# A fused two-layer network on one core: the triangle's b projection read by rows, its output in four row groups, gate logits joined, and the whole order drawn up anew

## The chip, the cores and the metric

The kernel runs on one core of a Trainium2 chip. A core has five engines that run their own queues of instructions in order: TensorE (PE) multiplies matrices and transposes, with its weight loads shown apart as PEld; VectorE (DVE) and ScalarE (ACT) work on tiles; GpSimd (POOL) here issues indirect DMAs; SyncE (SP) issues most other DMAs. Matmuls write to PSUM, which has eight banks of 512 floats per partition. The metric is the time of one execution in microseconds on the device. Before the change three runs took 4004.34 to 4016.94 us, with a median of 4013.66.

## The reference

The input x has 32 images of 56 x 56 pixels with 128 channels. Everything is float32. Two layers follow each other, each with a mixing part and an expert part, both added to x.

```python
x = x + conv3x3(sign(batchnorm(ln(x))), sign(W) * scale)   # layer 0
t = t + moe8_top2(ln(t))                                   # 8 experts of 128x128, two per token
# layer 1, the "triangle", with n = ln(x), per image:
a = sigmoid((n @ Wa1 + ba1) * (n @ Wa2 + ba2))             # 16 channels
b = sigmoid((n @ Wb1 + bb1) * (n @ Wb2 + bb2))
z = einsum('bikc,bkjc->bijc', a, b)
x = x + sigmoid(n @ Wg + bg) * (ln(z) @ Wz + bz)
# 64 experts, each picks its 8 best tokens of an image
probs = softmax(ln(t) @ gate_w.T + gate_b, over tokens)
topv, topi = top_k(probs, 8)
pooled = sum_k topv[k] * ln(t)[topi[k]]                    # one row per image and expert
o = gelu([pooled, 1] @ weight1) @ weight2                  # 128 -> 512 -> 128
t[topi[k]] += topv[k] * o                                  # scatter
```

## The kernel before

A first sweep reads all of x in 112 units of 896 tokens (7 per pair of images), normalizes, and collects the batch norm's sums. After that the kernel works by pairs of images: 16 pairs, each 7 units of 16 image rows, two half units of 8 rows (448 pixels) in each.

Per unit it runs the convolution (nine taps, `ps_cv`, L595), the eight small experts (`acc`, L794, on gates broadcast by SP and multiplied by DVE at L789), and a normalized, transposed copy `yT` of the pair. Transposes of all kinds go through one helper, `turned` (L439).

Then comes the triangle, once per pair. `gated_half` (L839) projects `yT` for a and for b: two halves, two images, four column groups of 32 outputs. For a the moving operand is seven whole image rows. For b it is seven image columns, so that consecutive elements lie a row (56 floats) apart. Each makes one PSUM bank (`ps_a`, `ps_b`) of 392 columns, read out by ACT (L846). After a transpose and the product of both projections, `tri_z` multiplies a and b per channel (`ps_z`, L929) and normalizes. Its result `zT` has, on 128 partitions, eight neighbouring image columns times 16 channels.

`tri_out` works per unit. It makes the gate (`ps_g`, L992, a sigmoid on ACT, L1002) and the output projection `ps_zo` (L1020): eight matmuls, four in each of two row groups of 64 partitions, against weights `wz_bd` in which only 16 rows of each block are not zero. Two PSUM banks receive them, each with four image columns. Two DVE instructions of 448 elements (L1030) add the bias and multiply by the gate.

Gate logits (L1084) come in seven chunks of 448 tokens per image; two images go side by side in one bank, with 64 experts each. Chunks 0 and 6 were split by image, so that nine PE steps served a pair. Then `top8` finds each expert's tokens on DVE (L1111, L1115), POOL gathers their rows (L1153), and `pool_rows` sums them.

The 64 large experts run in 16 groups of four at the end. A group loads about 2 MB of weights, does three PE steps (`ph` L1338, `trh` L1351, `po` L1365), spreads the result to tokens (`pe` L1391), multiplies by the gains on DVE (`eo`, L1400), and POOL scatters it: four experts times two lots of images, one indirect DMA each (L1417). A scatter must wait for the one before it in its lot. The first `LATE` groups run before the last pair is pooled, without it ("False" in tile names), and again alone for the last pair ("True"); the other groups run once for all.

No loop fixes the order of instructions. Every stage declares operations with an engine, an estimated duration in ns, and what they read and write. A planner in Python (`Order.run`) simulates the engines and picks for each the ready operation of the lowest rank; the emitted order is then fixed. Rank is a tick given in `plan` (`put`, `late`), 14 ticks to a pair. `AHEAD` limits how far a tile may run ahead of its turn for a buffer, `SPARE` how many must be left over.

Of the kernel before, what the change touches and what calls it, by code (L numbers as in the profile page):

```python
# [54 lines left out]
class Order:  # L55
# [11 lines left out]
    AHEAD = {"u": 14, "ps": 32}  # L67
# [64 lines left out]
    def run(self):  # L132
# [18 lines left out]
        def can(k):  # L151

            need = {}
            for t in ops[k][5]:
                if t not in slot:
                    need.setdefault(t.args[1], []).append(t)
            for tag, tiles in need.items():
                spare = sum(1 for f in free[tag] if f <= now) - len(tiles)
                if tag not in heads:
                    heads[tag] = list(  # L160
                        itertools.islice(
                            (t for t in self.queue[tag][turn[tag] :] if t not in slot),
                            self.AHEAD.get(tag, 6),
                        )
                    )
                head = heads[tag]

                if spare < (0 if set(head[: len(tiles)]) == set(tiles) else self.SPARE.get(tag, 1)):
                    return False
                if any(t not in head for t in tiles):  # L170
                    return False
            return True

        def pick(e):

            kept, best = [], None
            while ready[e]:
                item = heapq.heappop(ready[e])
# [5 lines left out]
                kept.append(item)  # L184
            for item in kept:
                if item is not best:
                    heapq.heappush(ready[e], item)
# [5 lines left out]
        while len(out) < n:  # L193
# [47 lines left out]
            while events and events[0][0] <= now:  # L241
                k = heapq.heappop(events)[1]
                if k >= 0:
                    heapq.heappush(ready[ops[k][0]], (ops[k][6], k))
# [9 lines left out]
def kernel(ctx: ExitStack, tc: tile.TileContext, a: dict, out: bass.AP):  # L254
# [40 lines left out]
    wz_bd = const.tile([128, NV // 2, C], F32, name="wz_bd")  # L295
# [77 lines left out]
    with ExitStack() as c2:  # L373
# [54 lines left out]
        def turned(src, name, keys=None, get=None):  # L428
# [4 lines left out]
            for n0, k in ((0, 4), (4, 3)):  # L433
                ps = bank(f"{name}_{n0}")

                @op("PE", k * 109, r=keys or parts(src)[n0 : n0 + k], w=[ps])
# [144 lines left out]
        def conv(p, u):  # L581
            g = p * NU + u
            cv = live[p]["cv", u] = unit_tile(f"cv_{g}")
            for h in range(2):
# [5 lines left out]
                @op("PE", 9 * 194, r=near, w=[ps])  # L590
# [59 lines left out]
        def moe_route(p, m):  # L650
# [12 lines left out]
            @op("PE", 870, r=[k for xT in xTs for k in parts(xT)], w=[psl])  # L663
# [14 lines left out]
            @op("PE", 440, r=[rT], w=[psr])  # L678
# [93 lines left out]
        def moe_experts(p, u, n):  # L772
# [18 lines left out]
            @op("PE", 222 * E0, r=[gb], w=[(acc, n % 4)])  # L791
# [37 lines left out]
        def gated_half(p, x, h, pieces, w, bias):  # L829


            name = f"{x}_{p}_{h}"
            for img in range(2):
                ps = bank(f"ps_{name}_{img}")

                @op("PE", 760, r=all_rows, w=[ps])
                def _(ps=ps, img=img):
                    for g in range(4):
                        nc.tensor.matmul(  # L839
                            ps.ap[32 * g : 32 * g + 32, :392].rearrange("s (i k) -> s i k", i=7),  # L840
# [4 lines left out]
                def _(ps=ps, img=img):  # L845
                    nc.scalar.activation(  # L846
                        lines[h][:, :, 64 * img : 64 * img + H],
                        ps.ap[:, :392].rearrange("s (i k) -> s i k", i=7),
# [24 lines left out]
        def tri_b(p, h):  # L873

            if h == 0:
# [4 lines left out]
                lambda img, g: yT[:, H * img : H * img + H, 14 * g + 7 * h : 14 * g + 7 * h + 7]  # L880
                .rearrange("c k j -> c j k"), wb, bb,
# [1007 lines left out]
```

## Time and profile before

| | |
|---|---|
| median of three runs | 4013.66 us |
| the profiled execution | 4013.14 us |
| its span, first to last instruction | 4011.4 us |
| mean granted PE clock | 0.960 |
| busy: PE, DVE, ACT, POOL | 3678.5, 3143.3, 2348.2, 418.2 us |
| ps_b, 512 matmul instructions | 102.0 us busy |
| ps_a, 512 matmul instructions | 60.7 us busy |
| ps_zo, 1792 matmul instructions | 130.6 us busy |
| gate logits, 448 matmul instructions | 131.1 us busy |
| gate product on DVE, 224 instructions | 150.2 us busy, 680 ns each |
| scatters on POOL, 128 | 198.9 us busy, 1554 ns each |

A float32 matmul shows as two instructions, so 512 instructions of ps_b are 256 matmuls. Busy time of a group is the union of its instructions; they overlap on PE, so that the mean length of one is longer than its share. A line of groups ends with the idle time just ahead of it and with whom the engine waited for. A time such as 3570.05 is counted from the start of the span.

### The profile page before, as it was taken

To read this page: it belongs to the slowest core of one execution; us is meant where nothing else is said; L and a number is where in the kernel's file an instruction comes from. 1 tells how busy PE (TensorE), PEld (TensorE's weight loads), DVE (VectorE), ACT (ScalarE), POOL (GpSimd) and SP (SyncE) were. 2 spreads that over 40 slices of the span, in tenths; PEclk is the share of its full clock that TensorE was granted. 3 is DMA by queue.
4 is the path that set the end of the run, shared out by engine and by line. 5 is a ranking of instruction groups with operands and counts; after the bars stand their busy time and mean duration, and the time that the engine had idled before them with its cause. 6 is when DMAs were issued, how large, how long until landed. Compare 5 with 4: busy or idle time off the path is not lost.

```text
span 4011.4 us, 78057 instructions
## 1 busy us (share of the span) xinstructions
PE 3678.5 (92%) x27747; PEld 2896.2 (72%) x27747; DVE 3143.3 (78%) x10284; ACT 2348.2 (59%) x5461; POOL 418.2 (10%) x441
## 2 busy tenths in 40 slices
PE   6998999999999999999999999999999999988574
PEld 6886877777777777776877777777778686865352
DVE  7997878797978797978888989797888788865310
ACT  5997347475656565656666665656474756555210
POOL 1000000101010001010101010101000101004655
PEclk8999999999999999999999999999999999988687
DMA  7996546373746464645555555555555555457685
GB/s 241 349 353 230 213 143 251 132 263 130 256 139 238 148 246 149 235 155 202 193 193 192 198 195 194 189 195 193 198 181 210 185 206 186 175 183 223 178 246 130
DMA packets 316805, 814.11 MB, mean 203 GB/s; under 512 B 72168, under 2 KB 96608, under 8 KB 316416
## 3 DMA queue, kind: packets, MB, share of 16 engines
q1 hardware_dynamic: 253296, 682.59, 49.0%
q10 hardware_dynamic: 41104, 109.20, 6.9%
q0 software_dynamic: 22016, 17.32, 2.8%
q8 instruction: 221, 3.62, 0.4%
q14 instruction: 168, 1.38, 0.1%
HBM read 638.78 MB, written 170.13 MB: 202 GB/s over the span
## 4 chain that ended last, share of the span: by engine, by line
PE 65%; ACT 10%; DMA 10%; DVE 8%; POOL 3%; issue 3%; SPq 1%; ACTq 0%; POOLq 0%; DVEq 0%
PE acc L794 31%; PE ps_cv L595 6%; DMA out<-eo_False,picked 4%; PE gram L1593 3%; PE ps_g L992 2%; PE ps_zo L1020 2%; PE ps_b L839 2%; PE ps_l L1084 2%; DMA rows<-y,near 2%; PE tr L439 2%; DMA gb<-gate 2%; ACT yt L524 2%; PE tro L439 2%; DVE gb L789 2%; PE trm L439 2%
## 5 line engine op out<-in xcount | busy, mean ns | idle before, releaser
L794 PEld LDWEIGHTS acc<-expert_w,gb 128*128 128x128 f32 x12544 | 1448.6, 195 | 99.7 <-DVE gb L789 32.0
L794 PE MATMUL acc<-expert_w,gb 128*128 128x128 f32 x12544 | 1471.8, 279 | 48.8 <-DVE gb L789 37.8
L789 DVE TENSOR_TENSOR gb<-gb,xT 128x1024 f32<-128x1024 f32 x784 | 944.3, 1221 | 80.1 <-DMA gb<-gate 73.9
L450 DVE BATCH_NORM_STATS2 stln<-x 128x6 f32<-128x128 f32 x2352 | 589.3, 286 | 2.5
L1153 POOL DMA_INDIRECT rows<-y,near x128 | 185.9, 1452 | 3396.6 <-PE trm L439 1681.0
L595 PE MATMUL ps_cv<-frame,w_sign 128*128 128x448 bf16 x2016 | 419.0, 356 | 7.1 <-DVE frame L573 7.1
L524 ACT ACTIVATE yt<-x,rmln 128x128 f32<-128x128 f32 x784 | 322.5, 484 | 160.7 <-DVE rmln L509 157.6
L524 ACT ACTIVATE ym<-x,rmln 128x128 f32<-128x128 f32 x784 | 326.8, 490 | 95.0 <-DVE rmln L512 81.4
L524 ACT ACTIVATE yl<-x,rmln 128x128 f32<-128x128 f32 x784 | 326.9, 486 | 33.6 <-DVE rmln L509 18.3
L595 PEld LDWEIGHTS <-w_sign 128*128 128x128 bf16 x2016 | 193.5, 98 | 185.7 <-issue 21.0
L603 ACT ACTIVATE cv<-ps_cv,cv_shift,cv_scale 128x448 f32<-128x448 f32 x224 | 161.4, 723 | 99.3 <-PE ps_cv L595 93.1
L1417 POOL DMA_INDIRECT out<-eo_False,picked x128 | 198.9, 1554 | 179.3 <-DMA out<-eo_False,picked 108.1
L545 ACT COPY xT<-trm 128x512 f32<-128x512 f32 x224 | 112.1, 542 | 179.5 <-PE trm L439 145.5
L524 ACT ACTIVATE y<-x,rm 128x128 f32<-128x128 f32 x448 | 195.2, 491 | 24.8 <-DVE rm L509 11.8
L806 DVE TENSOR_TENSOR x<-acc,x 128x512 f32<-128x512 f32 x224 | 139.4, 622 | 77.2 <-PE acc L794 76.5
L992 PE MATMUL ps_g<-yT,wg 128*128 128x448 f32 x448 | 199.6, 554 | 0.0
L1593 PE MATMUL gram<-y 128*128 128x128 f32 x1568 | 199.5, 281 | 0.0
L545 ACT COPY ylT<-trl 128x512 f32<-128x512 f32 x224 | 111.4, 534 | 147.2 <-PE trl L439 141.8
L1593 PEld LDWEIGHTS gram<-y 128*128 128x128 f32 x1568 | 195.9, 201 | 0.0
L450 DVE BATCH_NORM_STATS2 st<-x 128x6 f32<-128x128 f32 x784 | 180.0, 280 | 16.6 <-DMA x<-in_x 16.0
L1030 DVE SCALAR_TENSOR_TENSOR sg<-ps_zo,bz,sg 128x448 f32<-128x448 f32 x224 | 150.2, 680 | 43.4 <-PE ps_zo L1020 40.6
L1002 ACT ACTIVATE sg<-ps_g,bg 128x448 f32<-128x448 f32 x224 | 137.3, 634 | 69.2 <-PE ps_g L992 39.2
(229 smaller groups left out, 5449.8 us busy)
## 6 DMA issues: line engine op xcount, KB each, us to landing
gb<-gate SPq DMA_DIRECT2D x784, 512.0 KB
x<-in_x SPq DMA_DIRECT2D x224, 448.0 KB
y<-yT SPq DMA_DIRECT2D x112, 448.0 KB
ys<-y SPq DMA_DIRECT2D x112, 448.0 KB
out<-x ACTq DMA_DIRECT2D x112, 448.0 KB
y<-yl ACTq DMA_DIRECT2D x112, 448.0 KB
w_False<-in_L_ffn_weight SPq DMA_DIRECT2D x128, 256.0 KB
w_True<-in_L_ffn_weight SPq DMA_DIRECT2D x80, 256.0 KB
```

Source lines behind the costliest of these rows:

```text
L439: nc.tensor.transpose(ps.ap[:, n * 128 : (n + 1) * 128], get()[:, n0 + n, :], ident)
L450: nc.vector.bn_stats(st.ap[:, c0 + k, :], src.ap[:, k, :])
L524: nc.scalar.activation(dst.ap[:, k, :], src.ap[:, k, :], AF.Identity, bias=m, scale=r)
L545: nc.scalar.copy(t.ap[:, n0 : n0 + k, :].rearrange("c n p -> c (n p)"), ps.ap[:, : k * 128],)
L595: nc.tensor.matmul(acc, lhsT=w_sign[:, tap, :], rhs=frames[f][:, 8 * band + kh : 8 * band + kh + 8, kw : kw + W], start=(tap == 0), stop=( ...
L603: nc.scalar.activation(cv.ap[:, :, 64 * h : 64 * h + 64], ps.ap[:, :448].rearrange("c (q n) -> c n q", n=N7), AF.Identity, bias=cv_shift, ...
L789: nc.vector.tensor_tensor(gb.ap, gb.ap, over(xT.ap[:, n, :], E0), ALU.mult)
L794: nc.tensor.matmul(acc.ap[:, n % 4 * C : (n % 4 + 1) * C], lhsT=gb.ap[:, e, :], rhs=expert_w[:, e * C : (e + 1) * C], start=(e == 0), stop ...
L992: nc.tensor.matmul(psg.ap[:, :448], lhsT=wg, rhs=yT[:, H * img + r0 : H * img + r0 + 8, :].rearrange("c r w -> c (r w)"), start=True, stop ...
L1153: nc.gpsimd.indirect_dma_start(out=rows.ap[:, j, :], out_offset=None, in_=y3_d[p], in_offset=bass.IndirectOffsetOnAxis(ap=near.ap[:, k + j ...
L1417: ins = nc.gpsimd.indirect_dma_start(out=tokens_out, out_offset=bass.IndirectOffsetOnAxis(ap=picked[lot][:rows, e : e + 1], axis=0), in_=e ...
L1593: nc.tensor.matmul(gram.ap[:, :C], lhsT=y.ap[:, n, :], rhs=y.ap[:, n, :], start=(g % G16 == 0 and n == 0), stop=(g % G16 == G16 - 1 and n ...
```

## The change

The change has five parts.

1. For b, `gated_half` reads image rows of seven neighbouring columns (56 runs of seven floats) instead of seven columns. The bank's columns then come in another order, and ACT's readout turns them back.
2. `ps_zo` is split in four row groups of 32 partitions with a bank each: again eight matmuls, two in each group. DVE's product becomes four instructions of 224 elements.
3. Chunk 0 of the gate logits is done for both images at once.
4. The estimated PE durations are longer, but for `ps_zo`'s; POOL's indirect DMAs are estimated slower; `AHEAD` is smaller; most ticks move, and the late ticks of the last pair are scaled by 0.94.
5. `LATE` is 6 instead of 10, with other ticks for the late groups.

The planner's bookkeeping is rewritten too (a sorted list in place of a heap, an earlier test of `AHEAD`).

```diff
-    AHEAD = {"u": 14, "ps": 32}
+    AHEAD = {"u": 12, "ps": 31}
...
-                @op("PE", k * 109, r=keys or parts(src)[n0 : n0 + k], w=[ps])
+                @op("PE", k * 125, r=keys or parts(src)[n0 : n0 + k], w=[ps])
...
-                @op("PE", 9 * 194, r=near, w=[ps])
+                @op("PE", 9 * 200, r=near, w=[ps])
...
-            @op("PE", 870, r=[k for xT in xTs for k in parts(xT)], w=[psl])
+            @op("PE", 1100, r=[k for xT in xTs for k in parts(xT)], w=[psl])
...
-            @op("PE", 222 * E0, r=[gb], w=[(acc, n % 4)])
+            @op("PE", 227 * E0, r=[gb], w=[(acc, n % 4)])
...
-                @op("PE", 760, r=all_rows, w=[ps])
+                @op("PE", 830, r=all_rows, w=[ps])
                 def _(ps=ps, img=img):
                     for g in range(4):
                         nc.tensor.matmul(
-                            ps.ap[32 * g : 32 * g + 32, :392].rearrange("s (i k) -> s i k", i=7),
+                            ps.ap[32 * g : 32 * g + 32, :392].rearrange(
+                                "s (i k) -> s i k", k=7 if cols else H
+                            ),
                             lhsT=w, rhs=pieces(img, g), start=True, stop=True,
...
-                        ps.ap[:, :392].rearrange("s (i k) -> s i k", i=7),
+                        ps.ap[:, :392].rearrange("s (k i) -> s i k" if cols else "s (i k) -> s i k", i=7),
...
-                lambda img, g: yT[:, H * img : H * img + H, 14 * g + 7 * h : 14 * g + 7 * h + 7]
-                .rearrange("c k j -> c j k"), wb, bb,
+                lambda img, g: yT[:, H * img : H * img + H, 14 * g + 7 * h : 14 * g + 7 * h + 7],
+                wb, bb,
...
-            psz = [bank(f"ps_zo_{name}_{h}") for h in range(2)]
-
-            @op("PE", 4 * 230, r=[(zT, 0), (zT, 4), (sg, "s", 0)], w=psz)
+            psz = [bank(f"ps_zo_{name}_{q}") for q in range(4)]
+
+            @op("PE", 750, r=[(zT, 0), (zT, 4), (sg, "s", 0)], w=psz)
...
-                for v in range(4):
-                    for h in range(2):
-                        k = slice(64 * h, 64 * h + 64)
-                        acc = psz[h].ap[:, :448].rearrange(
-                            "c (n r v) -> c v n r", n=N7, v=4
+                for v in range(2):
+                    for q in range(4):
+                        k = slice(32 * q, 32 * q + 32)
+                        acc = psz[q].ap[:, :224].rearrange("c (n r v) -> c v n r", n=N7, v=2)
+                        nc.tensor.matmul(
+                            acc[:, v], lhsT=wz_bd[k, v, :], rhs=z_[k], start=True, stop=True,
+                            **({"tile_position": (96, 0)} if q == 3 else {}),
                         )
...
-            for h in range(2):
-                @op("DVE", 600, r=[psz[h], (sg, "s", 0), (sg, "s", 1)],
+            for q in range(4):
+                @op("DVE", 320, r=[psz[q], (sg, "s", 0), (sg, "s", 1)],
...
-            ((0, (1,)), (6, (0,))), ((0, (0,)), (1, (0, 1))), ((2, (0, 1)), (3, (0, 1))),
+            ((6, (0,)),), ((0, (0, 1)), (1, (0, 1))), ((2, (0, 1)), (3, (0, 1))),
...
-        LATE = 10
+        LATE = 6
...
-                        "POOL", 1500, land=2400,
+                        "POOL", 1650, land=2900,
...
+        SHRINK = {NP - 2: 1, NP - 1: 0.94}
...
-                    put(t + 0.15 * n, moe_experts, p, u, n)
+                    put(t + 0.05 * n, moe_experts, p, u, n)
...
-                put(16.5 + 0.53 * u, tri_turn, p, u)
+                put(16.67 + 0.53 * u, tri_turn, p, u)
...
-                put(20.09 + 0.2 * h, tri_b, p, h)
+                put(19.99 + 0.2 * h, tri_b, p, h)
...
-            t = 22.99
+            t = 22.81
...
-                    t += 0.84
+                    t += 1.02
...
-            put(t + 3.83, top8, p)
-            put(t + 7, pool_rows, p)
+            put(t + 3.51, top8, p)
+            put(t + 6.06, pool_rows, p)
+        first_at, last_at = (at(p, t + 7) for p in (NP - 2, NP - 1))
...
             if g < LATE:
-                late(t + 7.5 + 0.5 * g, late_experts, True, g)
-        late(t + 7.4, last_sums)
-        late(t + 14, last_out_rows)
+                late(first_at + 0.5 + 1.35 * g, late_experts, False, g)
+                late(last_at + 0.1 + 1.53 * g, late_experts, True, g)
+            else:
+                late(last_at + 0.1 + 0.68 * (g - LATE), late_experts, False, g)
```

## The prediction

> **What bounds the kernel now.** I read the page's busy shares and slices first. TensorE (PE) is busy 92% of the span, 9 tenths in nearly every slice at nearly full clock, until the last four slices, where it drops and GpSimd (POOL) rises.
>
> ```profile
> PE 3678.5 (92%) x27747; PEld 2896.2 (72%) x27747; DVE 3143.3 (78%) x10284; ACT 2348.2 (59%) x5461; POOL 418.2 (10%) x441
> PE   6998999999999999999999999999999999988574
> POOL 1000000101010001010101010101000101004655
> PEclk8999999999999999999999999999999999988687
> ```
>
> Then busy time by stretch. The first gather of pooled rows marks each pair of images: pair 0 at 705.2 us, pair 14 at 3570.05, so a pair costs 2864.85/14 = 204.6 us. The rows below (stretch, length, busy us of PE, PEld, DVE, ACT, POOL, clock, DMA share, GB/s) are this steady part, the last pair up to its own gathers (A), its gathers (B), the rest (C).
>
> ```profile
> 705.20:3570.05 2864.85, 2740.16 (x21032) 2164.09 (x21030) 2424.64 (x7499) 1750.82 (x3914) 167.94 (x112) 0.98 0.54 192
> 3570.00:3762.00 192.00, 150.65 (x945) 96.20 (x946) 83.74 (x262) 92.50 (x173) 86.90 (x104) 0.84 0.72 205
> 3762.00:3805.00 43.00, 16.13 (x71) 9.39 (x68) 14.37 (x28) 3.03 (x4) 33.44 (x40) 0.60 0.66 171
> 3805.00:4011.40 206.40, 119.45 (x761) 81.46 (x761) 26.88 (x65) 18.96 (x33) 118.76 (x161) 0.81 0.70 184
> ```
>
> Per pair, PE works 195.7 us of 204.6, DVE 173.2: PE is the bound, with 8.9 us idle. In C nothing on PE is near full. There the chain of waits is made of the indirect scatters of expert outputs; each waits for the one before in its lot, and two lots alternate.
>
> Last I read prices in the chain of waits (start, us, what). It runs over the lines the change edits.
>
> ```profile
> 3406.26 1.56 PE ps_b L839 x8
> 3407.82 1.32 PE ps_a L839 x16
> ...
> 3427.61 3.51 PE ps_z L929 x32
> ...
> 3446.74 1.08 PE ps_zo L1020 x16
> ...
> 3545.74 0.90 PE ps_l L1084 x4
> ```
>
> A bank of ps_b costs 1.56 us for 8 instructions; ps_a does two banks in 1.32, so 0.66 each with the same sizes. A unit of ps_zo costs 1.08.
>
> **The change, part by part.**
>
> ps_b (64 banks: 16 pairs, 2 halves, 2 images). Now the moving operand steps a whole image row (224 B) per element; ps_a reads contiguous rows. After, it reads runs of seven floats. No row has such runs. Bounds: 0.66 (free) and 1.56 (no gain). I take 0.75, nearest ps_a, because six of seven steps are contiguous: 0.81 x 64 = 52 us (0 to 58). [...]
>
> ps_zo (112 units). ps_z loads 128 weight columns per instruction and streams only 56: 3.51/32 = 110 ns, so weight loads set its pace. ps_zo, 16 instructions in two row groups, takes eight steps of 110 plus about 0.2 of fill, which is its 1.08: two row groups do run side by side. Four groups of 32 rows make four steps: 0.44 + 0.2 = 0.64 if they too run together, as ps_a's four column groups do. Upper bound 1.08. I take 0.68: 0.40 x 112 = 45 us (0 to 49). [...] No run here has four row groups.
>
> Gate logits. Chunk 0 now comes as one pair of images: eight PE steps per pair instead of nine. A lone image streams as long as two side by side (0.90 row, about 0.75 back to back): 12 us over the run (10 to 14). ACT loses 16 activations of 0.63; it has room.
>
> DVE. The product with the gate becomes four instructions of 224 instead of two of 448 (680 ns, starting 0.60 apart when queued). An element costs about 1.04 ns by this kernel's PSUM additions (691 ns at 512, 555 at 384), so 224 comes to 0.36: 4 x 0.36 - 2 x 0.60 = +0.24 per unit, 1.7 us per pair (0 to 3). Hidden where PE leads. It isn't everywhere: in the stretch from 2440 to 2540 us DVE is busy 93 of 100 us. With 1.7 more and at best 97% busy that stretch lasts 97.6, where PE's part of the gain (ps_zo 2.8, logits 0.75) would have given 96.5. I take off 1.1 x 15 = 16 us.
>
> ACT reads ps_b's bank with a stride of seven floats: 590 ns for 392 now, 634 for 448 in the sigmoid with that stride. At most 0.05 x 64 = 3 us, under ACT's 59%.
>
> The order. Longer PE durations, smaller look-ahead and other ticks move nearly every instruction on every engine. Steady PE work stays the same, so order can only move PE's idle: 15 x 8.9 = 133 us at most to win, and as much could come. I take zero and keep 50 each way. ps_zo now needs four of eight banks free at once; on PE's order other work (ps_g, transposes) stands between most units.
>
> The tail. Six instead of ten groups of late experts run before the last pair is pooled, and ten after. Passes over the weights fall from 26 to 22, but after the last pooling there are 16 both before (6 joined, 10 alone) and after (10 joined, 6 alone): the same 2 MB each. What grows in C is scatters. Here are POOL's, and the DVE queue in A (start, us, what, [idle before <- whom]).
>
> ```profile
> 3857.68 1.55 POOL L1417 DMA_INDIRECT out<-eo_False,picked  x1 [4.46 <-DMA out<-eo_False,picked]
> ...
> 3954.27 1.56 POOL L1417 DMA_INDIRECT out<-eo_False,picked  x1 [0.27 <-issue]
> ...
> 3981.56 1.56 POOL L1417 DMA_INDIRECT out<-eo_False,picked  x1 [0.27 <-issue]
> 3983.42 1.49 POOL L1417 DMA_INDIRECT out<-eo_False,picked  x1 [0.27 <-issue]
> ```
>
> ```profile
> 3747.03 0.69 DVE L1400 TENSOR_TENSOR eo_False<-pe_False,gains 128x512 f32<-128x512 f32 x1 [22.13 <-DMA out<-eo_False,picked]
> 3748.82 0.69 DVE L1400 TENSOR_TENSOR eo_False<-pe_False,gains 112x512 f32<-112x512 f32 x1 [1.10 <-DMA out<-eo_False,picked]
> 3749.43 3.42 DVE L1111 MAX8 m<-lgT 128x8 f32<-128x3136 f32 x1
> ```
>
> While weights stream, 30 scatters take 96.6 us, 3.2 each; without them 1.83.
>
> A: the last pair's top-8 sat behind an eo step that waited for scatters; PE had finished the logits at 3736. After, one group and that eo step fewer stand ahead: 13 us, and this pair's own 7 on PE: -20 (0 to -32). B: 14 scatters stood between the first and the last of the eight gathers, six do after; at 1.85 each -15 (-5 to -20). C: 80 scatters remain after pooling. Group 6 reaches POOL some 20 us after the transpose; weights take 114 us (93% DMA share from 3840 to 3954), which covers 36 scatters at 3.2; 44 more at 1.83 are 81 us; the last pair's own eight rows on POOL and the end, 12: 227 against 206, +21 (-28 at 1.83 throughout, +82 at 3.2). SP's queue holds the loads of joined groups two ahead of their scatters, so loads wait for scatters rather than the reverse. Sum of the tail: -14.
>
> **Sum.** For pairs 0 to 14: (52+45+12) x 15/16 = 102, less 16 = 86. Span 4011.4 - 86 - 14 = 3911; the profiled execution took 1.7 us more than its span and lies 0.5 under the median of 4013.7, so the forecast is 3914 us.
>
> **The rivals.**
> DVE takes over. If PE's gain is halved by DVE in its dense half (93 of 100) and by chains between PE and ACT, 51 stays of 102: 3950. For it: DVE is over 90% in eight of the ten slices of 10 us there. Against: over a pair DVE has 31 us of room.
>
> Order helps too. If half of PE's idle goes, -67: 3850. Against: waits on PE are many and short, none over 18 us.
>
> The tail grows. 80 scatters at 3.2 with nothing won in A and B: 4014 - 86 + 82 = 4010; halfway to the forecast's tail, 3962. For it: A already runs at 72% DMA share. Against: the loads are no more than before.
>
> Four banks at once stall PE (the slower side). PE stands in order; if a ps_zo waits for the four products of the unit before, 4 x 0.36 = 1.44 us per unit, 112 units lose 161, and 3914 + 161 = 4075. It decides from 100/112 = 0.9 us per unit on. Against: DVE's waits for ps_zo total 40 us now, PE's for DVE's products 3.2.
>
> The edits gain nothing: ps_b stays 1.56 and ps_zo 1.08; only logits and tail count: 4014 - 12 - 14 = 3988.
>
> **How the numbers follow.** Chances: forecast 0.56 (3875 to 3945), DVE 0.15, order 0.10, tail 0.09, stall 0.07, nothing 0.03. Faster by over 0.3% (12 us, what a measurement here can tell): all but the stall and bits of the tail and of the rest, 0.88; within, 0.04; slower, 0.08. The range from 3845 to 3985 leaves out the stall, half of the order case's lower part and the worst tail.
>
> **What would show it.** Busy time of ps_b from 102.0 to about 55 us; of ps_zo from 130.6 to about 85; logits 131.1 to 117; PE in all near 3547 (109 less, and four alone passes of some 5.4, their ph, trh and po). Pair distance near 199. The product's rows at 0.44 each, about 165 us together. C near 227 with scatters at its end 1.83 apart. It is wrong if ps_zo's matmuls start 110 ns apart, if PE waits for the products, or if PE's idle per pair leaves 8.9 by more than 3 us.

## The result and the profile after

The changed kernel takes 3967.8 us (median; 3960.4 to 3974.1), beside 4012.4 us for the kernel before on the same chip. The ratio is 0.9888, with an interval of 0.9867 to 0.9909: 45 us less, where 100 were forecast. The profiled execution has a span of 3958.7 us, 52.7 less than that of before; it was the fastest of the four, so that the stretches below add up to some 8 us more than the medians give.

The page's busy shares of the kernel after, and its slices for PE:

```profile
PE 3579.1 (90%) x27571; PEld 2832.1 (72%) x27571; DVE 3205.5 (81%) x10496; ACT 2318.1 (59%) x5435; POOL 411.9 (10%) x441
...
PE   7998999999999999999999999999999999988563
```

PE's work fell by 99 us, DVE's rose by 62, and the span fell by half of what PE lost. Of the 62 us, 30 are the four products in place of two (150.2 to 180.1 in their row); the rest is spread over many rows, by 3 us or less in each. Next is busy time by stretch of the kernel after, cut as in the prediction: the 14 steady pairs, the last pair up to its gathers (A), its gathers (B), the rest (C). The columns are the stretch, its length, then PE, PEld, DVE, ACT and POOL busy, clock, DMA share and GB/s.

```profile
696.72:3545.12 2848.40, 2692.66 (x21152) 2137.72 (x21149) 2495.89 (x7717) 1734.11 (x3909) 167.08 (x112) 0.98 0.57 195
3545.00:3707.00 162.00, 115.82 (x704) 68.01 (x704) 69.03 (x238) 85.87 (x165) 63.70 (x81) 0.82 0.64 180
3707.00:3731.00 24.00, 0.00 (x0) 0.00 (x0) 12.06 (x26) 1.25 (x2) 20.00 (x23) 0.50 0.33 51
3731.00:3958.70 227.70, 127.81 (x777) 88.32 (x777) 30.56 (x71) 20.33 (x34) 150.18 (x201) 0.73 0.70 173
```

| stretch | before | after | change | forecast |
|---|---|---|---|---|
| up to the first gather | 705.2 | 696.7 | -8.5 | in the next row |
| 14 pairs | 2864.9 | 2848.4 | -16.5 | -86 with the row above |
| A | 192.0 | 162.0 | -30 | -20 |
| B | 43.0 | 24.0 | -19 | -15 |
| C | 206.4 | 227.7 | +21.3 | +21 |

The tail came out at -27.7 us where -14 was forecast. The steady part, in which nearly all of the forecast gain lay, gave 25 us of 86. Its rows follow, from the groups of PE instructions of the kernel after (line, operation, count, busy us, mean ns of one, idle time just ahead of them and whom it waited for):

```profile
L438 PE MATMUL trl<-ident,yl 128*128 128x128 f32 x784 | 138.5, 290 | 12.7 <-ACT yl L523 9.9 <-DVE lg L711 0.9
L1085 PE MATMUL ps_l<-ylT,gate_w 128*64 128x448 f32 x448 | 123.2, 568 | 4.7 <-ACT ylT L544 4.6
L438 PE MATMUL trt<-ident,yt 128*128 128x128 f32 x784 | 121.2, 282 | 13.4 <-ACT yt L523 12.7
...
L438 PE MATMUL tro<-ident,sg 128*128 128x128 f32 x784 | 114.7, 287 | 35.4 <-DVE sg L1031 15.2 <-DVE q_ln L503 9.9 <-DVE rmln L508 7.5
...
L1021 PE MATMUL ps_zo<-zT,wz_bd 32*128 32x112 f32 x1792 | 91.1, 306 | 2.6 <-DVE x L536 1.7 <-DVE sg L1031 0.9
...
L840 PE MATMUL ps_b<-yT,wb 128*32 128x392 f32 x512 | 58.7, 541 | 1.4 <-ACT yT L817 1.3
L840 PE MATMUL ps_a<-yT,wa 128*32 128x392 f32 x512 | 57.9, 496 | 0.0
```

The three groups that the change was to make cheaper did get cheaper: ps_b 102.0 to 58.7, ps_zo 130.6 to 91.1, logits 131.1 to 123.2 us, 91 together. The same groups of the kernel before:

```profile
L1020 PE MATMUL ps_zo<-zT,wz_bd 64*128 64x112 f32 x1792 | 130.6, 283 | 3.1 <-DVE x L537 3.0
L439 PE MATMUL trt<-ident,yt 128*128 128x128 f32 x784 | 126.0, 287 | 39.8 <-ACT yt L524 38.5
...
L439 PE MATMUL trl<-ident,yl 128*128 128x128 f32 x784 | 117.5, 279 | 3.3 <-ACT yl L524 1.6 <-DVE k L697 0.9
...
L439 PE MATMUL tro<-ident,sg 128*128 128x128 f32 x784 | 106.1, 275 | 4.6 <-DVE sg L1030 3.2 <-ACT ym L524 1.3
L839 PE MATMUL ps_b<-yT,wb 128*32 128x392 f32 x512 | 102.0, 896 | 0.0
```

The same 784 transposes `trl` now show 21 us more busy time, and `tro` 9 more. Two things lengthen such a row without more work. A transpose can wait for its input while the one before it is still in the pipeline; counted from the starts of neighbours in the trace, such waits within `trl` grew from 7 to 19 us. And the drawn order breaks the transposes into more pieces, 182 instead of 146, each of which shows the length of a whole transpose at its end: in the timeline of PE seven in a row take 0.93 us, while four and three take 0.60 and 0.49. Not every row moved this way, since ahead of `trt` PE waits 26 us less than before. Ahead of `tro` it now waits 31 us more, and ahead of another group of transposes, `trg`, 19 more (22.3 instead of 3.8), mostly for DVE. The page's costliest groups show who waits for whom, first in the kernel before and then in the kernel after:

```profile
L794 PE MATMUL acc<-expert_w,gb 128*128 128x128 f32 x12544 | 1471.8, 279 | 48.8 <-DVE gb L789 37.8
L789 DVE TENSOR_TENSOR gb<-gb,xT 128x1024 f32<-128x1024 f32 x784 | 944.3, 1221 | 80.1 <-DMA gb<-gate 73.9
```

```profile
L793 PE MATMUL acc<-expert_w,gb 128*128 128x128 f32 x12544 | 1460.7, 278 | 56.0 <-DVE gb L788 51.3
...
L788 DVE TENSOR_TENSOR gb<-gb,xT 128x1024 f32<-128x1024 f32 x784 | 944.9, 1221 | 102.4 <-DMA gb<-gate 95.5
...
L1031 DVE SCALAR_TENSOR_TENSOR sg<-ps_zo,bz,sg 128x224 f32<-128x224 f32 x448 | 180.1, 450 | 13.3 <-PE ps_zo L1021 13.3
```

PE waits for DVE's gated tokens 51.3 us (37.8 before), and DVE waits for their DMA 95.5 us (73.9). ACT waits 205.3 us for the means that DVE makes for `yl` (18.3), but its idle time in all did not grow (1640.6 us, 1663.2 before), so this wait only moved there from other rows. PE's idle time in the whole span grew from 332.9 to 379.6 us: a part of what was saved on PE is now spent waiting. Last, one unit's four products and scatters near the end, from the timelines of DVE and POOL of the kernel after (start, us, what, idle before):

```profile
2463.16 1.53 DVE L1031 SCALAR_TENSOR_TENSOR sg<-ps_zo,bz,sg 128x224 f32<-128x224 f32 x4 [0.25 <-PE ps_zo L1021]
```

```profile
3939.38 1.57 POOL L1418 DMA_INDIRECT out<-eo_False,picked  x1 [0.22 <-issue]
...
3941.25 1.49 POOL L1418 DMA_INDIRECT out<-eo_False,picked  x1 [0.26 <-issue]
...
3943.04 1.00 POOL L1531 DMA_INDIRECT out<-last_rows,at_last  x1 [0.27 <-issue]
...
3944.35 1.57 POOL L1418 DMA_INDIRECT out<-eo_False,picked  x1 [0.22 <-issue]
```

### The profile page after: what moved, and what is told of

It is laid out like the page before. It is cut to its first block, busy times and chain, and to the rows that moved or that the text cites. A ratio compares the mean times of both kernels' runs of the same rounds, so it can differ in the third digit from the quotient of the medians.

```text
span 3958.7 us, 77662 instructions
## 1 busy us (share of the span) xinstructions
PE 3579.1 (90%) x27571; PEld 2832.1 (72%) x27571; DVE 3205.5 (81%) x10496; ACT 2318.1 (59%) x5435; POOL 411.9 (10%) x441
## 5 line engine op out<-in xcount | busy, mean ns | idle before, releaser
L793 PE MATMUL acc<-expert_w,gb 128*128 128x128 f32 x12544 | 1460.7, 278 | 56.0 <-DVE gb L788 51.3
L793 PEld LDWEIGHTS acc<-expert_w,gb 128*128 128x128 f32 x12544 | 1433.5, 194 | 99.1 <-DVE gb L788 65.2
L788 DVE TENSOR_TENSOR gb<-gb,xT 128x1024 f32<-128x1024 f32 x784 | 944.9, 1221 | 102.4 <-DMA gb<-gate 95.5
L523 ACT ACTIVATE yl<-x,rmln 128x128 f32<-128x128 f32 x784 | 326.3, 492 | 213.2 <-DVE rmln L508 205.3
L1031 DVE SCALAR_TENSOR_TENSOR sg<-ps_zo,bz,sg 128x224 f32<-128x224 f32 x448 | 180.1, 450 | 13.3 <-PE ps_zo L1021 13.3
L438 PE MATMUL tr<-ident,y 128*128 128x128 f32 x784 | 140.6, 297 | 29.7 <-ACT y L523 24.6
```

The source lines that it names most:

```text
L438: nc.tensor.transpose(ps.ap[:, n * 128 : (n + 1) * 128], get()[:, n0 + n, :], ident)
L523: nc.scalar.activation(dst.ap[:, k, :], src.ap[:, k, :], AF.Identity, bias=m, scale=r)
L788: nc.vector.tensor_tensor(gb.ap, gb.ap, over(xT.ap[:, n, :], E0), ALU.mult)
L793: nc.tensor.matmul(acc.ap[:, n % 4 * C : (n % 4 + 1) * C], lhsT=gb.ap[:, e, :], rhs=expert_w[:, e * C : (e + 1) * C], start=(e == 0), stop ...
L1031: nc.vector.scalar_tensor_tensor(part, psz[q].ap[:, :224].rearrange("c (m v) -> c m v", v=2), bz, part, ALU.add, ALU.mult,)
```

## The experiments

Each ratio is to the kernel before on the same chip, with its 95% interval. A difference of 0.0025 in the ratio is 10 us. To compare two kernels I subtract their ratios and multiply by 4012 us; the interval of such a difference is about 11 to 17 us each way, so that single differences of 8 to 18 us below are at the edge of what can be told or under it. The steady part is measured here over the 13 pairs from the first gather to that of pair 13, because pair 14 already shares its time with the late groups. Over these the kernel before takes 204.7 us a pair with PE busy 196.3, and the kernel after 202.5 with PE busy 191.7.

The theories: PE passes on what it saves, and a term of the sum was mis-sized (the prediction's own); DVE is a bound beside PE, so that its additional work eats the gain; the order that the planner draws sets the time; or, as the first results came in, several in-order engines and the chains between them set the time in turn.

### The b projection alone

The kernel before, reading b by rows. The order of all instructions stays as it was.

```diff
...
-                lambda img, g: yT[:, H * img : H * img + H, 14 * g + 7 * h : 14 * g + 7 * h + 7]
-                .rearrange("c k j -> c j k"), wb, bb,
+                lambda img, g: yT[:, H * img : H * img + H, 14 * g + 7 * h : 14 * g + 7 * h + 7],
+                wb, bb,
```

> The kernel before with the b projection read by rows alone; estimates and so the order of every instruction are those of before. The changed kernel's trace prices this part at 43 us of PE busy time (102.0 to 58.7). Theory P (PE is the bound and its savings reach the time; what is missing in the changed kernel was lost by the new order): 35 to 43 us faster, some 3972. Theory D (a second bound, DVE or the chains between PE, ACT and DVE, takes half or more of what PE saves): 10 to 22 us faster, some 3996.

Measured: 3984.6 us, 0.9956 (0.9942 to 0.9971), 18 us less. The row of ps_b fell from 102.0 to 65.7 us, and with its order untouched PE passed on half of that. DVE's work and the order are as before here, so neither more work on DVE nor a new order is needed to lose half of a saving.

```profile
L840 PE MATMUL ps_b<-yT,wb 128*32 128x392 f32 x512 | 65.7, 573 | 0.0
```

### The split product alone

The kernel before, with each product of 448 elements issued as two of 224 from the same bank.

```diff
-                    nc.vector.scalar_tensor_tensor(
-                        part,
-                        psz[h].ap[:, :448].rearrange("c (m v) -> c m v", v=4),
-                        bz, part, ALU.add, ALU.mult,
-                    )
+                    src = psz[h].ap[:, :448].rearrange("c (m v) -> c m v", v=4)
+                    for v0 in (0, 2):
+                        nc.vector.scalar_tensor_tensor(
+                            part[:, :, v0 : v0 + 2], src[:, :, v0 : v0 + 2],
+                            bz, part[:, :, v0 : v0 + 2], ALU.add, ALU.mult,
+                        )
```

> The kernel before with the product on DVE issued as four instructions of 224 elements instead of two of 448, the order otherwise that of before; PE work is unchanged. DVE is busy 1.7 to 4 us longer per pair. Theory P: DVE has room, 0 to 6 us slower. Theory D: DVE's time counts in its dense stretch, 15 to 45 us slower.

Measured: 4019.3 us, 1.0038 (1.0027 to 1.0048), 15 us more. DVE is busy 3166.9 us instead of 3143.3: of 24 us more work on an engine that is 78% busy, 0.6 reached the time. DVE is not hidden under PE.

### The computation without the plan, and the plan without the computation

First, the kernel before with the three edits of the computation (b by rows, `ps_zo` in four row groups with four products, joined logits), but the old ticks, `LATE`, `AHEAD` and estimates; `ps_zo` is declared with 920 ns and a product with 300.

```diff
...
-            psz = [bank(f"ps_zo_{name}_{h}") for h in range(2)]
+            psz = [bank(f"ps_zo_{name}_{q}") for q in range(4)]
-            @op("PE", 4 * 230, r=[(zT, 0), (zT, 4), (sg, "s", 0)], w=psz)
+            @op("PE", 920, r=[(zT, 0), (zT, 4), (sg, "s", 0)], w=psz)
...
-                @op("DVE", 600, r=[psz[h], (sg, "s", 0), (sg, "s", 1)],
+                @op("DVE", 300, r=[psz[q], (sg, "s", 0), (sg, "s", 1)],
...
-            ((0, (1,)), (6, (0,))), ((0, (0,)), (1, (0, 1))), ((2, (0, 1)), (3, (0, 1))),
+            ((6, (0,)),), ((0, (0, 1)), (1, (0, 1))), ((2, (0, 1)), (3, (0, 1))),
```

> The three edits of the computation (b by rows, output in four row groups and banks, logits joined) with the ticks, look-ahead, LATE and estimates of before (the output 920 for PE and four times 300 for DVE); the planner draws its order from these. Theory P with a costly new order: 70 to 95 us faster than before, so faster than the changed kernel. Theory D: 35 to 55 us faster, as the changed kernel, since the second bound is there under any order.

Measured: 4064.0 us, 1.0145 (1.0127 to 1.0163), 58 us more, where both theories had expected less time. Then the kernel after with the three edits undone, but its plan kept; `ps_zo` is declared with 1100 ns.

```diff
...
-            psz = [bank(f"ps_zo_{name}_{q}") for q in range(4)]
+            psz = [bank(f"ps_zo_{name}_{h}") for h in range(2)]
-            @op("PE", 750, r=[(zT, 0), (zT, 4), (sg, "s", 0)], w=psz)
+            @op("PE", 1100, r=[(zT, 0), (zT, 4), (sg, "s", 0)], w=psz)
...
-                @op("DVE", 320, r=[psz[q], (sg, "s", 0), (sg, "s", 1)],
+                @op("DVE", 600, r=[psz[h], (sg, "s", 0), (sg, "s", 1)],
...
-            ((6, (0,)),), ((0, (0, 1)), (1, (0, 1))), ((2, (0, 1)), (3, (0, 1))),
+            ((0, (1,)), (6, (0,))), ((0, (0,)), (1, (0, 1))), ((2, (0, 1)), (3, (0, 1))),
```

> The computation of before with the ticks, look-ahead, LATE and estimates of the changed kernel (the output in two row groups estimated at 1100, its product at 600). Theory P with a costly new order: 20 to 50 us slower than before. Theory D: within 15 us of before; the tail alone, from the traces, would be 15 to 28 us faster.

Measured: 3948.2 us, 0.9860 (0.9843 to 0.9878), 56 us less than before, which again neither theory had. The plan alone gives no less than the whole change does; the three edits under it cost 11 us net, which is also the size of the uncertainty. The stretches of the 13 pairs and from pair 13 to pair 15 of this kernel:

```profile
695.97:3323.31 2627.34, 2548.53 (x19638) 1997.81 (x19636) 2286.31 (x7019) 1620.96 (x3647) 140.04 (x105) 0.99 0.56 197
3323.31:3684.62 361.31, 314.39 (x2251) 229.94 (x2251) 244.05 (x732) 205.33 (x432) 79.64 (x88) 0.93 0.60 191
```

A pair takes 202.1 us (2627.34/13) with PE busy 196.0: the plan does with less waiting (6.1 us of PE's idle per pair instead of 8.4) what the kernel after does with less work. From pair 13 to pair 15 it takes 361 us, where the kernel before takes 396 and the kernel after 378. So the 56 us are not all order in the steady part: the profiled executions differ by 71, of which 9 lie ahead of the first gather, 33 in the 13 pairs and 29 behind them, in the part that the forecast counts as tail.

The 58 us of the first kernel lie in the 13 pairs, which take 2736.7 us instead of 2660.8, while its other stretches together take 26 us less than before. PE is idle 12.8 us per pair there instead of 8.4, and busy 197.7 instead of 196.3 although its three groups are cheaper. What these 58 us are made of is not settled: b by rows and the split product alone cost -18 and +15, but the four banks, the logits and the order, which is drawn anew with the old ticks, were not parted from each other there.

### The output in two row groups under the new plan

The kernel after, with `ps_zo` as it was before (two row groups, two banks, two products), declared with 1100 and 600 ns. The order is drawn anew.

```diff
-            psz = [bank(f"ps_zo_{name}_{q}") for q in range(4)]
+            psz = [bank(f"ps_zo_{name}_{h}") for h in range(2)]
-            @op("PE", 750, r=[(zT, 0), (zT, 4), (sg, "s", 0)], w=psz)
+            @op("PE", 1100, r=[(zT, 0), (zT, 4), (sg, "s", 0)], w=psz)
...
-                @op("DVE", 320, r=[psz[q], (sg, "s", 0), (sg, "s", 1)],
+                @op("DVE", 600, r=[psz[h], (sg, "s", 0), (sg, "s", 1)],
```

> The changed kernel with the output projection put back to two row groups, two banks and two products of 448 (estimates 1100 and 600), the rest as changed; the planner draws its order anew. Theory D (PE and DVE bound together: before, 43 us less on PE gave 20 and 24 us more on DVE cost 15): the four row groups save 40 us of PE at a price on DVE that eats it, so this is as fast as the changed kernel or faster, 3920 to 3960; with the plan's kernel at 3948 and the b projection's 20, some 3930. Theory P: 25 to 40 us slower than the changed kernel, 3990 to 4010.

Measured: 3938.4 us, 0.9826 (0.9789 to 0.9862), 70 us less than before and ahead of both kernels. Two groups of PE of this kernel:

```profile
L793 PE MATMUL acc<-expert_w,gb 128*128 128x128 f32 x12544 | 1453.9, 277 | 21.3 <-DVE gb L788 19.6 <-DVE mk L695 0.5 <-DVE rmln L474 0.4
...
L438 PE MATMUL tro<-ident,sg 128*128 128x128 f32 x784 | 108.4, 275 | 3.9 <-DVE sg L1033 2.7 <-DVE rmln L479 0.7
```

PE is busy longer, but it waits 21 us ahead of `acc` instead of 56, and 4 ahead of `tro` instead of 35. This could be the form's merit or the order's, so the next runs part them.

### Order and form apart

Without a change of the order: the kernel after with its four banks and four products, but with the matmuls in two row groups.

```diff
-                for v in range(2):
-                    for q in range(4):
-                        k = slice(32 * q, 32 * q + 32)
-                        acc = psz[q].ap[:, :224].rearrange("c (n r v) -> c v n r", n=N7, v=2)
+                for v in range(4):
+                    for h in range(2):
+                        k = slice(64 * h, 64 * h + 64)
+                        acc = psz[2 * h + v // 2].ap[:, :224].rearrange(
+                            "c (n r v) -> c v n r", n=N7, v=2
+                        )
...
-                            acc[:, v], lhsT=wz_bd[k, v, :], rhs=z_[k], start=True, stop=True,
-                            **({"tile_position": (96, 0)} if q == 3 else {}),
+                            acc[:, v % 2], lhsT=wz_bd[k, v, :], rhs=z_[k], start=True, stop=True,
```

> The changed kernel, its order and its four products unchanged, but the eight matmuls of the output run in two row groups (each of their banks is written by one of them), so that PE pays 1.08 again instead of about 0.7: 40 us more PE. Theory D: 10 to 25 us slower than the changed kernel. Theory P: 35 to 45 us slower.

Measured: 3973.5 us, 0.9907 (0.9875 to 0.9938), 8 us more than the kernel after, while the row of ps_zo grew from 91.1 to 141.2 us and PE's busy time in all by 38. With 15 us of uncertainty each way, theory P's 35 to 45 are out, and a gain from nothing to 23 us is left.

```profile
L1023 PE MATMUL ps_zo<-zT,wz_bd 64*128 64x112 f32 x1792 | 141.2, 296 | 1.0 <-DVE x L536 0.6 <-DVE sg L1032 0.3
```

The four row groups run side by side as meant, and little of what they save on PE reaches the time here.

Only the order: the kernel after, with the planner told the product's measured pitch.

```diff
-                @op("DVE", 320, r=[psz[q], (sg, "s", 0), (sg, "s", 1)],
+                @op("DVE", 358, r=[psz[q], (sg, "s", 0), (sg, "s", 1)],
```

> The changed kernel with one estimate changed: the product of 224 at 358 ns, its measured pitch, instead of 320. Only the planner's order changes. Theory O (the order was drawn on a DVE that is too fast, so DVE runs late and PE waits): 10 to 30 us faster than the changed kernel. Otherwise within 15 us, the scatter between orders.

Measured: 3978.8 us, 0.9926 (0.9903 to 0.9949), 15 us more. A truer estimate made it no faster, so this run gives no support to theory O; it is one drawn order, and not more. The two-row-group kernel with its product declared with 650 instead of 600 ns is the same kind of redrawing in the other form:

```diff
-                @op("DVE", 600, r=[psz[h], (sg, "s", 0), (sg, "s", 1)],
+                @op("DVE", 650, r=[psz[h], (sg, "s", 0), (sg, "s", 1)],
```

> The kernel with the output projection in two row groups and two products (3938 us when it was run), in which the planner is told 650 instead of 600 ns for a product: only the order changes, the computation does not. If the 30 us by which that form stood ahead of the kernel after belong to the form (two products of 448 cost DVE 24 us less than four of 224, two banks instead of four), it stays within 15 us of 3938. If they are the scatter of the orders, of which one change of an estimate gave 15 us in the kernel after, it may land anywhere from 3925 to 3985, and lands above 3955 as likely as not.

Measured: 3950.6 us, 0.9870 (0.9853 to 0.9886), 18 us more by the ratios. By the plain medians it is 12, but the kernel before, run beside each, took 4013.3 and 4002.6; so this lies at the border between the two cases. One number in the plan seems to move either form by 15 to 18 us, with 12 and 16 us of uncertainty. The mean of the two orders is 0.9848 for two row groups and 0.9907 for four, 24 us apart with a scatter of nearly that size. Two draws a form don't settle whether two row groups are better; nothing here shows the 40 us that four save on PE.

Only DVE: the two-row-group kernel with each product split in two, order unchanged (the edit is that of the split product above).

> The kernel with the changed plan, b by rows, logits joined and the output in two row groups (3938 us, ratio 0.983), its order unchanged, with each product of 448 issued as two of 224: 24 us more DVE, PE unchanged. Theory D: 5 to 20 us slower than that kernel, as it was 15 in the order of before. Theory P: 0 to 5 us.

Measured: 3956.5 us, 0.9857 (0.9838 to 0.9875), 12 us more for 24 us of DVE, by the middle as in the kernel before, though with 16 us of uncertainty. If the clearer 15 us of the kernel before are taken, the split that the four banks bring costs about what the four row groups save (8, with 15 of uncertainty).

### What a microsecond is worth on each engine

The next runs change the work of one engine and leave the order alone. The kernel after with b read by columns again:

```diff
-                lambda img, g: yT[:, H * img : H * img + H, 14 * g + 7 * h : 14 * g + 7 * h + 7],
-                wb, bb,
+                lambda img, g: yT[:, H * img : H * img + H, 14 * g + 7 * h : 14 * g + 7 * h + 7]
+                .rearrange("c k j -> c j k"), wb, bb,
...
```

> The changed kernel, its order unchanged, with the b projection streamed by columns again: 43 us more PE. Theory D (only a part of PE's time reaches the end; 0.42 of it in the order of before, 0.2 for the output): 8 to 22 us slower than the changed kernel. Theory P: 38 to 45 us slower.

Measured: 3991.1 us, 0.9933 (0.9910 to 0.9956), 18 us more; the row of ps_b is 98.7 instead of 58.7 us. That is the same 18 as in the kernel before, so that nothing shows the new plan to help or hinder this edit.

Seven of eight experts in PE's matmuls:

```diff
-                for e in range(E0):
+                for e in range(E0 - 1):
```

> The changed kernel, its order unchanged, with seven of the eight small experts in the matmuls (the eighth is left out of the sum): 1.8/8 us less PE in each of 784 steps, 10.9 us per pair, 175 us in all; DVE's work is unchanged. Theory D: DVE and the chains hold the rest, 25 to 75 us faster than the changed kernel, as 9 us less DVE per pair gave 40. Theory P: 110 to 170 us faster.

Measured: 3907.1 us, 0.9729 (0.9710 to 0.9747), 64 us less than the kernel after. The row of `acc` in this kernel tells where the rest is:

```profile
L793 PE MATMUL acc<-expert_w,gb 128*128 128x128 f32 x10976 | 1321.2, 281 | 123.5 <-DVE gb L788 104.8 <-issue 9.3 <-DVE q_ln L470 3.7
```

An eighth of 1460.7 is 183 us of work taken away. The row fell by 139.5, so that 43 stayed in its busy time, and the idle time ahead of it rose from 56.0 to 123.5. So 111 us were lost in this row, the idle part of them mostly as waits for DVE's gated tokens, and 72 of the 183 are left. By the ratios the time fell by 64 us, by the two profiled spans by 47 (3958.7 to 3911.4): most of what was lost is found in one row.

Half of the channels in DVE's statistics:

```diff
-                    nc.vector.bn_stats(st.ap[:, c0 + k, :], src.ap[:, k, :])
+                    nc.vector.bn_stats(st.ap[:, c0 + k, :], src.ap[:, k, :64])
```

> The changed kernel with its order, but the statistics of the layer norms read 64 of 128 channels (so normalization uses half of the channels): the 2352 + 784 of them cost DVE about 130 instead of 195 ns, so some 150 us less DVE after the first sweep, 200 in all; PE's work is unchanged. Theory D: half or more of the 10 us per pair come off the time, 60 to 110 us faster. Theory P: DVE has room, 0 to 15 us faster.

Measured: 3923.3 us, 0.9786 (0.9754 to 0.9819), 41 us less than the kernel after for 194 us less on DVE (3205.5 to 3011.7), between the two theories. DVE's load does hold the kernel back, but it passes on a fifth. Here DVE waits 122.1 us for the gates' DMA, up from 95.5.

Both of these edits together:

> The changed kernel, its order unchanged, with both: seven of eight experts and layer norm statistics over half of the channels. Theory D: the two cuts open each other, and the gain is more than the sum of the two alone, over 120 us. Theory P: the gain of the seven experts and no more than 15 us on top.

Measured: 3870.0 us, 0.9633 (0.9612 to 0.9653), 102 us less than the kernel after, for 64 + 41 = 105 by the sum. Neither theory is met: D asked for more than 120, since relieving both should have opened each for the other, and P for no more than 79. Of 377 us of work taken away on the two engines (183 and 194), 102 came through. That the gains simply add doesn't yet prove a further engine, since work that passes through PE and DVE in turn would add up as well.

So the last run adds work to ACT, which is 59% busy: two of seven activations of each normalized unit are issued twice.

```diff
-                        nc.scalar.activation(
-                            dst.ap[:, k, :], src.ap[:, k, :], AF.Identity, bias=m, scale=r
-                        )
+                        for _ in range(2 if engines == "AAAAAAA" and k in (2, 5) else 1):
+                            nc.scalar.activation(
+                                dst.ap[:, k, :], src.ap[:, k, :], AF.Identity, bias=m, scale=r
+                            )
```

> The kernel after, in which two of the seven activations of each normalized unit (ym, yt, yl) are issued twice with the same input and output: 672 more activations of about 0.39 us of queue each, 262 us of ACT in all, 16 us per pair on top of 124 of 202. The order is the same otherwise. Theory M (several in-order engines and the chains between them set the time in turn, ACT's chains among them; PE passes on about 0.4 of a saving and DVE about 0.2, so that some 0.4 is left for others): between 50 and 110 us longer than the kernel after, 4015 to 4080. Theory P (PE and DVE alone share the time, and ACT at 59% has slack): at most 15 us longer, 3983 or less.

Measured: 4130.7 us, 1.0320 (1.0303 to 1.0337), 173 us more than the kernel after, far above both expectations. ACT's busy time rose by 319 us (2318.1 to 2637.2), not by the 262 expected, and 0.54 of it reached the time. That is about what the split product showed for DVE (15 of 24) and the b projection for PE (18 of 36). This run adds work, and in a chain that PE waits for; what less work on ACT would give was not tried. Its PE groups:

```profile
L438 PE MATMUL trl<-ident,yl 128*128 128x128 f32 x784 | 152.9, 298 | 28.3 <-ACT yl L524 24.5 <-DMA y<-yl 0.4
L1086 PE MATMUL ps_l<-ylT,gate_w 128*64 128x448 f32 x448 | 137.9, 587 | 12.2 <-ACT ylT L545 11.4 <-DVE stln L449 0.7
L438 PE MATMUL trt<-ident,yt 128*128 128x128 f32 x784 | 133.7, 288 | 26.6 <-ACT yt L524 25.0
L438 PE MATMUL trm<-ident,ym 128*128 128x128 f32 x784 | 128.2, 282 | 20.0 <-ACT ym L524 17.9
```

Against the kernel after, the three transposes and the logits show 53.5 us more busy time without an instruction more (552.7 against 499.2), and 53.4 us more idle time ahead of them (87.1 against 33.7). The mean granted clock is lower here, 0.943 against 0.957, but it explains little of this: `acc`, with its 12544 matmuls unchanged, shows 1472.3 us against 1460.7, under 1% more. PE's share of busy time stays at 89% in a kernel that ACT has slowed by 4%.

## Why the prediction was wrong

The direction and the range held, the size did not: 100 us were forecast and 45 came. The step that failed is the sum for pairs 0 to 14, where "102, less 16" passed on PE's saving nearly whole, because "PE is the bound". In its place the runs show that, with the order untouched, 18 us came of 36 saved on PE by the b projection, and 8 of 50 by the four row groups. "I take zero" for the order failed as well, since the plan alone gave 56 us. Point by point:

- **What bounds the kernel.** "PE is the bound, with 8.9 us idle" was read from a busy share of 96% per pair. The runs show that PE passed on 0.2 to 0.5 of its own work (36 us to 18; 40 to 18; 50 to 8; 183 to 64), DVE 0.6, 0.5 and 0.2 (24 to 15; 24 to 12; 194 to 41), ACT 0.54 (319 to 173). Each engine's work counts partly; the shares from differences of 8 to 18 us are rough. PE's busy rows contain waits between pipelined instructions (7 us within `trl` in the trace of before, 19 in the kernel after), so that its idle time of 8.9 us isn't all its slack.
- **ps_b.** Forecast 52 us, measured 43.3 (102.0 to 58.7), and ps_b now costs what ps_a does (57.9), as the forecast's nearest row said. That row, 0.66 us for a bank, was read from two banks back to back, and 0.75 was taken after it; in the whole row a bank takes 58.7/64 = 0.92. The 0.75 was the author's estimate between the two rows of before, since no row had runs of seven floats; against whole rows they show 0.8 us more in 58 in the kernel after, and 4.0 more in the b projection alone (65.7 and 61.7).
- **ps_zo.** Forecast 45 us, measured 39.5. In the trace the matmuls of the four row groups start 7 ns apart, and one step follows the next after 112 ns, so they do run together, four steps to a unit; a unit takes 0.71 us against 1.08 or 1.15, where the forecast had 0.68. The step of 110 ns was read from `ps_z`; in the trace of before its matmuls start 112 ns apart, and 32 of its weight loads, which also start 112 ns apart, keep PEld busy for 3.65 us. The 5.5 us by which the gain fell short did not decide the time: with 50 us taken back the time rose by 8.
- **Logits.** Forecast 12 us, measured 8 (131.1 to 123.2).
- **DVE.** The size of the product was right: products start 0.36 us apart (1.53 us for four, the last one's latency with it) and cost 30 us more in their row (150.2 to 180.1), where 1.7 us a pair, 27 in all, was forecast. The 165 us that the prediction names for the row don't fit its own 27 (150.2 and 27 make 177). Its price was taken as 16 us, by one dense stretch; the two runs on the split alone cost 15 and 12. That the price came out right doesn't bear out the working, which let DVE count only where it is over 90% busy.
- **The order.** Priced at zero with 50 each way. The plan alone, tail included, gives 56 us; some 43 of the 71 between the profiled executions lie ahead of the tail. The new computation under the old ticks takes 58 us more, and how much of that is its order isn't known. A single estimate moves the time by 15 to 18. So the order is as large a term as any in the sum, and the trace of before had no row for it.
- **The tail.** A -30 for -20 and B -19 for -15, both in their ranges, and C +21.3 for +21. In C the size held by luck. The forecast had 36 scatters in 114 us of weights at 3.2 us each and 44 behind them at 1.83. In the kernel after the weights come until about 3885 us, 154 us into C (325 GB/s in the five us before it, 29 in the five behind), with scatters 2.8 apart up to 3892; only 25 scatters stand behind that. At the end they are 1.87 us apart, with one of the last pair's own (1.00 us) after every two.
- **The rivals.** None is the case as written. "DVE takes over" comes nearest: it halved PE's gain, by DVE and by chains between PE and ACT, and gave 3950 where 3968 came. Half is what the b projection lost, and work on DVE and ACT does count; but DVE alone isn't the second bound, since relieving it gives back only a fifth. "Four banks at once stall PE" did not come: PE waits 0.9 us ahead of ps_zo for products, in all.
- **What would show it wrong.** PE's idle time per pair went from 8.9 to 11.1 us ((2848.40 - 2692.66)/14), short of the 3 us that the text named. That threshold was too wide to notice 2.2 us a pair, or 35 in all, on a forecast of 86. Two other signs did show it: PE is busy 3579.1 us in all where 3547 was named, and a pair takes 203.5 us where 199 was.

Put together, 91 us less in three groups of PE are 5.7 a pair. Busy time fell by 4.6 (196.3 to 191.7 over the 13 pairs), and the distance by 2.2. As a ledger: the plan alone gives 56 us; b by rows and joined logits under it bring the kernel with two row groups to 70, near the 56 + 18 that the single runs name; and the four row groups with four banks and four products, with their own order, then take 25 back (17 each way). What remains open is how far that loss belongs to four banks and four products in particular, and how far to this one drawn order; the two forms differ by 24 us with a scatter of 15 to 18.

## What to carry to other kernels

A busy share of 96% on one engine doesn't say that its savings reach the time (here 18 us came of 36): before a saving is priced, take away or add a known amount of work on each engine with the order left alone, and use the share that comes through. In a kernel with a fixed order on several in-order engines, look for the saved time as waits in the rows of the next consumer, inside its busy time too (same count, longer row: `trl` here, 784 transposes, 117.5 to 138.5 us). Where a planner draws the order, price the redrawing as a term of its own, and part it from the computation with two runs, the computation alone and the plan alone.

## What the runs showed of the hardware

- A moving operand read in runs of seven floats costs PE nearly what whole rows cost (58.7 and 57.9 us for 512 instructions in the kernel after, 65.7 and 61.7 in the order of before); with single floats 224 B apart it costs 98.7 to 102.0.
- Four row groups of 32 partitions with a bank each start 7 ns apart, and the next four 112 ns later. The step is as long as that of two row groups (112 in the trace of before), so twice the groups took half the steps.
- Additional work on ACT, at 59% busy, was no cheaper here than on the fuller engines: 319 us of busy time cost 173, where 262 us had been expected to cost at most 110.
